# A recurrent kernel on one core: another order of loads, splits and first products in its opening

## The chip, the cores and the metric

The kernel runs on one core of a Trainium2 chip. A core has a matrix engine (TensorE, PE in the profile; PEld is its weight load), a vector engine (VectorE, DVE), a scalar engine (ScalarE, ACT), GpSimd (POOL) and SyncE (SP), which here only issues DMAs. The engines run side by side, each through its own instructions in order, and wait for each other by semaphores. The 16 DMA engines carry all transfers.

The metric is the device time of one execution in microseconds. The time before is 3092.99 us, the median of three runs (3092.69 to 3093.82).

## The reference

```python
xW = einsum('ntd,dh->nth', x, Wx) + b            # N=64 rows, T=256 steps, D=H=1024
h[t] = tanh(h[t-1] @ Wh + xW[t])                 # h[-1] = cond
x = x + h                                        # layer 0
s = silu(cond @ W1.T + b1)
gate = sigmoid(s @ W2.T + b2)                    # one gate per row and column
# layer 1: a Haar transform over t, each of its coefficients times gate, and back; + residual twice
y = x + (x + haar_back(haar(x) * gate))
```

The gate does not depend on t, so the transform and its inverse cancel and y = (x + h) * (2 + gate). This is what the kernel computes, all in float32.

## The kernel before, in words

**The recurrence.** The 256 steps depend on each other. Each step is one 64x1024 by 1024x1024 product with Wh, done as seven products of half size (Strassen's scheme in Winograd's form, `h_product`). Its factors on the side of Wh are four blocks as loaded and three differences: T5 (`first`), T6 (`second`, needs T5), T4 (`others`), and for the seventh product a difference T7 written over a block of Wh in place (`others` too, ahead of T4). They are built once, at step 0. In a step the order on TensorE is products 1, 2, 5, 6, 7, 4, 3, so T5, T6, T7 and T4 are needed in this order.

**The inputs' product.** x @ Wx is done for two steps (a pair, 128 rows) at a time. Float32 matmuls are slow, so x and Wx are split: high bits (x0, w0), the rest (x1, w1), and a mixed part (x2, w2), where x2 = x0 - 4096 x1 and likewise for w. Three products of the fast type fp32r, x0 w0 and x1 (4096 w1) into the banks `main`, x2 w2 into the banks `mixed`, together give the full one. `split_weight` makes the three parts of one 128x1024 block of Wx on VectorE and ScalarE: VectorE masks the high bits (line 118), subtracts them from the raw block in place (135) and makes w2 (137); ScalarE copies w0 (134) and scales w1 (136). `XWork` does the same for a pair of x, and holds the products: `block` for pair 1, block of Wx by block, and `first` and `second` for the later pairs. `take_mixed` brings `mixed` out of PSUM on ScalarE and adds the bias on GpSimd; `finish` adds `main` on VectorE (line 336) and sends the sum through DRAM to the layout of the steps (`xw`); `put` copies one step's `xw` into the bank in which the step accumulates (line 230, ScalarE).

**The opening.** Steps 0 and 1 have no pair product to lean on: `x_block` multiplies pair 0 by the raw Wx (plain float32, four column groups of 32), `h_block` adds cond @ Wh for step 0. Since `x_block(k)` reads the raw block k, the subtraction in place in `split_weight(k)` has to wait for it. Before that come four matmuls on a tile of zeros (`WARM`, line 380) that use no input. Around these stand the gate's first product, cond @ W1.T, in eight blocks (`plain_product` into `gate_ps`), and its second, from step 3 on.

**Who sets the order.** TensorE's order is the program's. Up to the end of step 1, VectorE's and ScalarE's orders are the program's too (`in_order`). SyncE and GpSimd are ordered by the scheduler of the framework. Tiles are reused: the raw blocks 0 to 5 of Wx, then the blocks 0 to 5 of W1, then T5, T6 and T4 lie in the same six tiles in turn (`sums_tile`). So a block of W1 is loaded when the raw block is done with, and a T is made when the gate's product with the block of W1 under it is done. A bank or tile with one buffer (`high`, `sum`, `acc`) is written again when its last reader is done; `hT` has two.

**Order on TensorE at the opening**: x_block 0 to 7, with block 0 of pair 1 after x_block 3 and block 1 after x_block 5; h_block 0 to 7; blocks 2 to 6 of pair 1; gate blocks 0 and 1; block 7; gate blocks 2 to 5; step 1's products 1, 2, 5, 6, 7; gate blocks 6 and 7; products 4, 3; then pair 2's `first`; then step 2.

Of the kernel before, what the change touches and what calls it, by code (L numbers as in the profile page):

```python
# [52 lines left out]
F32 = mybir.dt.float32  # L53
F32R = mybir.dt.float32r
I32 = mybir.dt.int32
AF = mybir.ActivationFunctionType
ALU = mybir.AluOpType

N, T, D = 64, 256, 1024
P = 128  # L60
R = 32
Q = P // R
B = D // P
G = N // R
F = D // Q
# [3 lines left out]
S = 2  # L69
NP = T // S  # L70
HALF = 512
HIGH = -(1 << 12)
UP = float(1 << 12)
DOWN = 1.0 / UP
WARM = 4
LATE = 3
AHEAD = 2
RINGS = 1024
# [3 lines left out]
def tile_cond_resid(  # L82
# [13 lines left out]
    nc = tc.nc  # L96
# [3 lines left out]
    split = ctx.enter_context(tc.tile_pool(name="split", bufs=1))  # L100
# [11 lines left out]
    def load_x(i: int) -> None:  # L112
        pairs[i] = slab(f"x{i}")
        nc.sync.dma_start(out=pairs[i], in_=xT[i])

    def high_bits(v, name: str):
        t = split.tile([P, D], I32, tag="high", name=name)
        nc.vector.tensor_scalar(out=t, in0=v.bitcast(I32), scalar1=HIGH, scalar2=None, op0=ALU.bitwise_and)
        return t[:].bitcast(F32)
# [4 lines left out]
    def load_weight(k: int):  # L124

        raw = sums_tile(f"wx{k}") if k < 3 * KB // 2 else slab(f"wx{k}")
        nc.sync.dma_start(out=raw, in_=wx[k])  # L127
        return raw

    def split_weight(raw, k: int) -> list:  # L130

        w0 = high_bits(raw[:], f"wx_high{k}")
        three = [wpool.tile([P, D], F32R, tag=f"wx{i}", name=f"wx{i}_{k}") for i in range(3)]
        nc.scalar.copy(three[0], w0)
        nc.vector.tensor_sub(raw, raw, w0)
        nc.scalar.activation(three[1], raw, AF.Copy, scale=UP)
        nc.vector.scalar_tensor_tensor(out=three[2], in0=raw, scalar=-UP, in1=w0, op0=ALU.mult, op1=ALU.add)
        return three

    def load_bias(v: bass.AP, pool, tag: str, name: str):  # L140
# [11 lines left out]
    class StrassenWeight:  # L152
# [20 lines left out]

            self.new(6, self.sides[3], self.sides[5])

        def others(self) -> None:

            b = self.sides
            for k in range(KB):
                nc.vector.tensor_sub(self.b12[k], b[3][k], self.b12[k])  # L180
            self.new(4, b[2], b[6])

    def strassen_product(out, a, i: int, first: bool = False) -> None:

# [13 lines left out]
    def plain_product(ps, vT, w, k: int, of=None, start: bool = True, stop: bool = True) -> None:  # L198

        for g in range(G):  # L200
            col = of(g) if of else (g * B + k) * R
            for q in range(Q):


                nc.tensor.matmul(  # L205
                    out=ps[q * R : (q + 1) * R, g * F : (g + 1) * F],
                    lhsT=vT[:, col : col + R],
                    rhs=w[:, q * F : (q + 1) * F],
                    start=start and k == 0 and g == 0,
                    stop=stop and k == B - 1,  # L210
                    skip_group_check=True,
                    tile_position=(0, q * R),
                )
# [19 lines left out]
    def h_product(acc, a: dict, t: int):  # L233

        m16, m57 = (bank(f"m{i}", f"m{i}_{t}") for i in (16, 57))
        m16, m5, m7 = m16[:, :E], m57[:, :E], m57[:, E : 2 * E]
        part = [acc[:, i * E : (i + 1) * E] for i in range(3)]
        y = sums.tile([P, 4, E], F32, tag="y", name=f"y{t}")
        u = sums.tile([P, E], F32, tag="u", name=f"u{t}")
        strassen_product(m16, a[1], 1, True)  # L240
        nc.scalar.copy(y[:, 0], m16)
        strassen_product(part[0], a[2], 2)
        strassen_product(m5, a[5], 5, True)
        strassen_product(m16, a[6], 6)
        nc.scalar.copy(u, m16)
        strassen_product(m7, a[7], 7)
        if t == 1:

            for k in range(B - 2, B):
                plain_product(gate_ps, h0T, w1[k], k)  # L250
        nc.vector.tensor_add(  # L251
            y[:, 1:3], m57[:, : 2 * E].rearrange("p (i e) -> p i e", i=2), u[:].unsqueeze(1).broadcast_to((P, 2, E))
        )
        nc.vector.tensor_add(y[:, 3], m7, y[:, 1])
        strassen_product(part[2], a[4], 4)
        strassen_product(part[1], a[3], 3)
        h = work.tile([P, W], F32, tag="h", bufs=1, name=f"h{t}")
        for v in pieces(t):
            nc.vector.tensor_add(h[:, v], acc[:, v], flat(y)[:, v])  # L259
        return h  # L260
# [6 lines left out]
    def bank(tag: str, name: str):  # L267
        return one_pool.tile([P, HALF], F32, tag=tag, name=name)

    def x_matmul(acc, v, which: int, h: int, k: int, start=False, stop=False) -> None:  # L270

        nc.tensor.matmul(  # L272
            out=acc[h],
            lhsT=v[:, k * P : (k + 1) * P],
            rhs=wx_s[k][which][:, h * HALF : (h + 1) * HALF],
            start=start and k == 0,
            stop=stop and k == B - 1,
        )

    class XWork:  # L280


        def __init__(self, i: int):

            self.i, x = i, pairs[i]
            self.high = high_bits(x[:], f"x_high{i}")
            self.x1 = split.tile([P, D], F32R, tag="x1", name=f"x1_{i}")
            nc.vector.tensor_sub(self.x1, x, self.high)  # L288
            self.x2 = split.tile([P, D], F32R, tag="x2", name=f"x2_{i}")
            nc.vector.scalar_tensor_tensor(  # L290
                out=self.x2, in0=self.x1[:].bitcast(F32), scalar=-UP, in1=self.high, op0=ALU.mult, op1=ALU.add
            )
# [22 lines left out]

        def first(self) -> None:
            self.begin()
            for h in range(2):
                for k in range(B):
                    x_matmul(self.mixed, self.x2, 2, h, k, True, True)  # L320
            self.take_mixed()
            for k in range(B):
                x_matmul(self.main, self.x1, 1, 0, k, start=True)

        def second(self) -> None:
            for k in range(B):
# [27 lines left out]

    h0T = const.tile([P, W], F32, tag="h0T", name="h0T")
    b_row = const.tile([P, D], F32, tag="b_row", name="b_row")
    load_x(1)
    pairs[0] = slab("x0")
    for part in (slice(0, HALF), slice(HALF, D)):
        nc.sync.dma_start(out=pairs[0][:, part], in_=xT[0][:, part])  # L360
        if part.start == 0:
            wx_raw = [load_weight(0)]
    wx_raw += [load_weight(k) for k in range(1, B)]
    nc.sync.dma_start(out=h0T, in_=condT)
    wx_s, wh_raw = [], []
    for k in range(B):
# [8 lines left out]
    in_order.enter_context(tc.manual_schedule(engines={mybir.EngineType.DVE, mybir.EngineType.Activation}))  # L375

    idle = const.tile([P, W], F32, tag="spare", name="idle")
    nc.gpsimd.memset(idle, 0.0)
    for _ in range(WARM):
        nc.tensor.matmul(out=bank("m16", "unused")[:, :F], lhsT=idle[:, :P], rhs=idle[:, :F], start=True, stop=True)  # L380
    now = XWork(1)
    now.begin()
    acc, acc1, gate_ps = bank("acc", "acc0"), bank("m57", "acc1_raw"), bank("gate", "gate_ps1")

    def x_block(k: int) -> None:
# [8 lines left out]
    def load_w1(k: int) -> None:  # L394
        w1.append(sums_tile(f"w1_{k}") if k < 3 * KB // 2 else slab(f"w1_{k}"))
        nc.sync.dma_start(out=w1[k], in_=w1T[k])

    def split_block(k: int) -> None:
        wx_s.append(split_weight(wx_raw[k], k))

    for k in range(B):
        x_block(k)
        split_block(k) if k < B - 1 else None
        if k in (3, 5):
            now.block(k // 4)
    for k in range(B - 1):
        load_w1(k)
    for k in range(B):
        h_block(k)
# [19 lines left out]
    def blocks(v):  # L429
        return v[:].rearrange("p (g b m) -> p g b m", g=G, b=B)  # L430
# [5 lines left out]
    def of_step(x, s: int):  # L436
        return x[:].rearrange("p (b s g m) -> p s g b m", b=B, s=S, g=G)[:, s]
# [31 lines left out]
    for t in range(T):  # L469
# [11 lines left out]
        if t == 0:  # L481
            acc = bank("acc", "acc1")
            nc.vector.tensor_add(acc, acc1, b_n)
            split_block(B - 1)
            load_w1(B - 1)
            for k in range(2, B):
                if k == B - 1:
                    for j in range(2):
                        plain_product(gate_ps, h0T, w1[j], j)
                now.block(k)  # L490
            now.take_mixed()
            wh_s = StrassenWeight(wh_raw)
            wh_s.first()
            wh_s.second()
            xw_next = now.finish()
            for k in range(2, B - 2):
                plain_product(gate_ps, h0T, w1[k], k)
            wh_s.others()
            later = XWork(2)


        elif s == 0:
            if i + 1 < NP:
                acc = put(xw[1], t + 1)
            if i + 2 < NP:
                now.second()
                if i + 3 < NP:
                    later = XWork(i + 2)
                xw_next = now.finish()
        if s == 1 and i + 3 < NP:  # L510
            now = later
# [18 lines left out]


        x = pairs[i]
        if t + S < T:
            nc.gpsimd.tensor_add(of_step(x, s), of_step(x, s), blocks(hT))  # L534
        if LATE <= t < LATE + B:
            k = t - LATE
# [78 lines left out]
```

## Time and profile before

| | us |
|---|---|
| median of three runs | 3092.99 |
| the profiled execution | 3094.69 |
| its span, from the first to the last instruction | 3092.8 |
| TensorE busy in the span | 3081.2 |
| VectorE busy | 1769.1 |
| step 1's first product starts at | 48.52 |
| pair 2's `first` starts on TensorE at | 59.05 |
| step 2's first product starts at | 64.75 |

The span starts at the first instruction of the core; all times below count from there. In a timeline each line is one group of like instructions: start, duration, engine, line of the kernel, operation, tile written, tiles read, shape and count, and in brackets the idle time of the engine before the group and what ended it. A float32 matmul appears as two records. TensorE is busy for all but some 12 us of the span, so what a change to the opening can alter is the time at which step 2 starts; from there on both programs have the same order on TensorE.

### The profile page before, as it was taken

Reading aid. Unit: us, or ns where it says so; the run is one execution under the profiler, and the core shown is the slowest. Engines: PE = TensorE matmul, PEld = TensorE weight load, DVE = VectorE, ACT = ScalarE, POOL = GpSimd, SP = SyncE. Lnnn points to the kernel's source line nnn. Section 1 sums busy time; section 2 is a strip of 40 time slices with the busy share of each in tenths; the row PEclk is TensorE's granted clock in tenths of the full one; section 3 lists DMA queues with packets and bytes.
Section 4 is the critical chain, followed back from the end, with each engine's and each line's share of the span. In section 5 each row is a group of like instructions: output and inputs, shape, how many; then the busy total and the mean of one; then the engine's idle time right before and its main releaser. Section 6 shows DMA issues by size and latency. Waiting matters only on the chain.

```text
span 3092.8 us, 138217 instructions
## 1 busy us (share of the span) xinstructions
PE 3081.2 (100%) x64072; PEld 2693.9 (87%) x64072; DVE 1769.1 (57%) x2739; ACT 713.7 (23%) x1420; POOL 1109.4 (36%) x765
## 2 busy tenths in 40 slices
PE   9999999999999999999999999999999999999999
PEld 6888888888888888888888888888888888888888
DVE  7555556555555555555555555555555555555556
ACT  3222222222222222222222222222222222222221
POOL 1233433343333343433333333333333333333332
PEclk9999999999999999999999999999999999999999
DMA  7332232232232322222222222222222222222221
GB/s 253 118 111 94 94 103 92 92 103 98 91 101 88 105 91 99 91 96 84 92 90 96 86 91 91 91 91 91 90 92 91 90 92 90 92 88 90 95 78 57
DMA packets 164034, 299.13 MB, mean 97 GB/s; under 512 B 44160, under 2 KB 110208, under 8 KB 163456
## 3 DMA queue, kind: packets, MB, share of 16 engines
q1 hardware_dynamic: 163168, 290.03, 27.3%
q8 instruction: 501, 8.21, 1.1%
q14 instruction: 77, 0.63, 0.1%
q10 hardware_dynamic: 288, 0.26, 0.0%
HBM read 154.40 MB, written 135.79 MB: 94 GB/s over the span
## 4 chain that ended last, share of the span: by engine, by line
PE 96%; DMA 2%; DVE 1%; SPq 0%; issue 0%; ACT 0%; DVEq 0%; ACTq 0%
PE main L272 30%; PE m L188 29%; PE acc L188 21%; PE mixed L272 15%; DMA w<-w1T 0%; PE acc L205 0%; DMA wh<-wh 0%; DMA wx<-wx 0%; DMA sum_d<-sum 0%; PE gate_ps L205 0%; DMA xw<-sum_d 0%; DMA b_n<-b 0%; DVE x L288 0%; SPq L127 0%; DVE hT L478 0%
## 5 line engine op out<-in xcount | busy, mean ns | idle before, releaser
L534 POOL TENSOR_TENSOR x<-x,hT 128x512 f32<-128x512 f32 x254 | 450.6, 1774 | 1751.6 <-DVE hT L478 1730.6
L272 PE MATMUL main<-wx,x 128*128 128x512 f32 x4032 | 973.4, 393 | 0.0
L272 PEld LDWEIGHTS main<-wx,x 128*128 128x128 f32 x4032 | 746.9, 188 | 177.0 <-issue 25.6
L251 DVE TENSOR_TENSOR y<-m,u 128x256 f32<-128x256 f32 x255 | 108.2, 424 | 847.8 <-PE m L188 847.8
L272 PE MATMUL mixed<-wx,x 128*128 128x512 f32 x2016 | 495.2, 397 | 1.6 <-DVE x L290 1.6
L188 PE MATMUL m<-t,s 128*32 128x128 f32 x16320 | 492.5, 273 | 0.2 <-DVE s L220 0.2
L272 PEld LDWEIGHTS mixed<-wx,x 128*128 128x128 f32 x2016 | 368.7, 188 | 98.8 <-issue 24.6
L188 PEld LDWEIGHTS m<-t,s 128*32 128x32 f32 x16320 | 450.8, 110 | 0.5 <-issue 0.4
L305 POOL TENSOR_TENSOR sum<-sum,b_row 128x512 f32<-128x512 f32 x252 | 325.3, 1292 | 197.3 <-ACT sum L304 197.3
L477 ACT ACTIVATE h<-h 128x512 f32<-128x512 f32 (+1 forms) x258 | 162.0, 629 | 794.9 <-DVE h L259 793.3
L440 POOL TENSOR_TENSOR x<-x,factor 128x512 f32<-128x512 f32 x244 | 330.5, 1354 | 15.4 <-DVE factor L426 5.7
L259 DVE TENSOR_TENSOR h<-acc,y 128x512 f32<-128x512 f32 (+1 forms) x257 | 176.5, 688 | 236.5 <-PE acc L188 236.3
L478 DVE STREAM_TRANSPOSE hT<-h 128x512 f32<-128x512 f32 (+1 forms) x258 | 182.4, 708 | 202.5 <-ACT h L477 202.5
L188 PEld LDWEIGHTS m<-wh,hT 128*32 128x32 f32 x8160 | 208.7, 109 | 87.3 <-issue 83.8
L290 DVE SCALAR_TENSOR_TENSOR x<-x,x_high 128x1024 fp32r<-128x1024 f32 x126 | 282.7, 2244 | 0.1
L188 PE MATMUL m<-wh,hT 128*32 128x128 f32 x8160 | 275.5, 275 | 0.0
L188 PE MATMUL acc<-wh,s 128*32 128x128 f32 x8160 | 271.1, 273 | 0.4 <-issue 0.4
L188 PE MATMUL m<-wh,s 128*32 128x128 f32 x8160 | 270.1, 273 | 0.4 <-DVE wh L180 0.4
L188 PE MATMUL acc<-t,hT 128*32 128x128 f32 x8160 | 270.2, 273 | 0.2 <-issue 0.2
L188 PE MATMUL acc<-wh,hT 128*32 128x128 f32 x8160 | 269.8, 273 | 0.3 <-ACT acc L230 0.2
L296 ACT CAST x<-x_high 128x1024 fp32r<-128x1024 f32 x126 | 131.9, 1047 | 465.4 <-PE main L272 462.5
L188 PEld LDWEIGHTS acc<-wh,s 128*32 128x32 f32 x8160 | 228.9, 110 | 1.1 <-issue 1.1
(59 smaller groups left out, 2354.0 us busy)
## 6 DMA issues: line engine op xcount, KB each, us to landing
x<-xT SPq DMA_DIRECT2D x127, 512.0 KB, 3.7
sum_d<-sum SPq DMA_DIRECT2D x126, 512.0 KB, 3.1
xw<-sum_d SPq DMA_DIRECT2D x1008, 64.0 KB, 2.0
yT<-x SPq DMA_DIRECT2D x122, 512.0 KB, 3.5
wx<-wx SPq DMA_DIRECT2D x8, 512.0 KB, 8.7
wh<-wh SPq DMA_DIRECT2D x8, 512.0 KB, 10.2
w<-w1T SPq DMA_DIRECT2D x8, 512.0 KB, 7.2
w<-w2T SPq DMA_DIRECT2D x8, 512.0 KB, 4.4
```

What stands on the lines that cost most here:

```text
L188: nc.tensor.matmul(out=out[q * R : (q + 1) * R], lhsT=a[:, k * R : (k + 1) * R], rhs=wh_s.sides[i][k][:, q], start=first and k == 0, stop= ...
L251: nc.vector.tensor_add(y[:, 1:3], m57[:, : 2 * E].rearrange("p (i e) -> p i e", i=2), u[:].unsqueeze(1).broadcast_to((P, 2, E)))
L259: nc.vector.tensor_add(h[:, v], acc[:, v], flat(y)[:, v])
L272: nc.tensor.matmul(out=acc[h], lhsT=v[:, k * P : (k + 1) * P], rhs=wx_s[k][which][:, h * HALF : (h + 1) * HALF], start=start and k == 0, s ...
L290: nc.vector.scalar_tensor_tensor(out=self.x2, in0=self.x1[:].bitcast(F32), scalar=-UP, in1=self.high, op0=ALU.mult, op1=ALU.add)
L296: nc.scalar.copy(self.x0, self.high)
L305: nc.gpsimd.tensor_add(s, s, b_row[:, h * HALF : (h + 1) * HALF])
L440: nc.gpsimd.tensor_mul(of_step(x, s), of_step(x, s), blocks(factor))
L477: nc.scalar.activation(h[:, v], h[:, v], AF.Tanh)
L478: nc.vector.transpose(hT[:, v], h[:, v])
L534: nc.gpsimd.tensor_add(of_step(x, s), of_step(x, s), blocks(hT))
```

## The change

It touches the opening only, in these parts.

- `split_weight` writes w - w0 to the tile of w1 and not over the raw block; the scaling by 4096 is then done in place on that tile, after w2 has been made from it.
- The loads start with block 0 of Wx, issued by ScalarE, and a quarter of pair 0 (before: a half) by SyncE; then block 1 of Wx, the rest of pair 0, pair 1, and the blocks 2 to 7 of Wx.
- The matmuls on zeros are five of 128 columns (before: four of 256), and VectorE writes the zeros (before: GpSimd).
- VectorE and ScalarE split block 0 of Wx first, then pair 1, then blocks 1 to 7; before, pair 1 came first and block 7 after step 0.
- All eight blocks of W1 are loaded ahead of b1 (before: the eighth after it).
- Gate blocks 0 to 3 stand ahead of block 7 (before: 0 and 1), 4 and 5 behind it (before: 2 to 5); 6 and 7 stay inside step 1.
- VectorE makes pair 2's high bits ahead of T5, then T5, T6, T7, then pair 1's sum (`finish`), then T4, then the rest of pair 2's split. Before: T5, T6, `finish`, T7, T4, the whole split.
- `first` of pair 2 begins with the eight matmuls of x1 into `main`, then the sixteen into `mixed`; before, and for all later pairs, it is the other way round.
- GpSimd's additions of h to x for steps 0 and 1 both stand at step 1. In the built order they follow the sums of pair 2, and the store of pair 0 moves behind five loads of b2.

```diff
-WARM = 4
+WARM = 5
...
-        nc.sync.dma_start(out=raw, in_=wx[k])
+        (nc.sync if k else nc.scalar).dma_start(out=raw, in_=wx[k])
...
         nc.scalar.copy(three[0], w0)
-        nc.vector.tensor_sub(raw, raw, w0)
-        nc.scalar.activation(three[1], raw, AF.Copy, scale=UP)
-        nc.vector.scalar_tensor_tensor(out=three[2], in0=raw, scalar=-UP, in1=w0, op0=ALU.mult, op1=ALU.add)
+        nc.vector.tensor_sub(three[1], raw, w0)
+        w1 = three[1][:].bitcast(F32)
+        nc.vector.scalar_tensor_tensor(out=three[2], in0=w1, scalar=-UP, in1=w0, op0=ALU.mult, op1=ALU.add)
+        nc.scalar.activation(three[1], w1, AF.Copy, scale=UP)
...
-        def others(self) -> None:
+        def third(self) -> None:
 
             b = self.sides
             for k in range(KB):
                 nc.vector.tensor_sub(self.b12[k], b[3][k], self.b12[k])
-            self.new(4, b[2], b[6])
+
+        def fourth(self) -> None:
+
+            self.new(4, self.sides[2], self.sides[6])
...
             self.high = high_bits(x[:], f"x_high{i}")
+
+        def split(self) -> None:
+
+            i, x = self.i, pairs[self.i]
             self.x1 = split.tile([P, D], F32R, tag="x1", name=f"x1_{i}")
...
         def first(self) -> None:
             self.begin()
+
+            def low() -> None:
+                for k in range(B):
+                    x_matmul(self.main, self.x1, 1, 0, k, start=True)
+
+
+            low() if self.i == 2 else None
             for h in range(2):
                 for k in range(B):
                     x_matmul(self.mixed, self.x2, 2, h, k, True, True)
             self.take_mixed()
-            for k in range(B):
-                x_matmul(self.main, self.x1, 1, 0, k, start=True)
+            low() if self.i > 2 else None
...
-    load_x(1)
+    wx_raw = [load_weight(0)]
     pairs[0] = slab("x0")
-    for part in (slice(0, HALF), slice(HALF, D)):
+    for part in (slice(0, 2 * P), slice(2 * P, D)):
         nc.sync.dma_start(out=pairs[0][:, part], in_=xT[0][:, part])
         if part.start == 0:
-            wx_raw = [load_weight(0)]
-    wx_raw += [load_weight(k) for k in range(1, B)]
+            wx_raw.append(load_weight(1))
+    load_x(1)
+    wx_raw += [load_weight(k) for k in range(2, B)]
...
-    nc.gpsimd.memset(idle, 0.0)
+    nc.vector.memset(idle[:, :P], 0.0)
     for _ in range(WARM):
-        nc.tensor.matmul(out=bank("m16", "unused")[:, :F], lhsT=idle[:, :P], rhs=idle[:, :F], start=True, stop=True)
-    now = XWork(1)
-    now.begin()
+        nc.tensor.matmul(out=bank("m16", "unused")[:, :P], lhsT=idle[:, :P], rhs=idle[:, :P], start=True, stop=True)
...
     for k in range(B):
         x_block(k)
-        split_block(k) if k < B - 1 else None
+        split_block(k)
+        if k == 0:
+            now = XWork(1)
+            now.split()
+            now.begin()
         if k in (3, 5):
             now.block(k // 4)
-    for k in range(B - 1):
+    for k in range(B):
         load_w1(k)
...
             nc.vector.tensor_add(acc, acc1, b_n)
-            split_block(B - 1)
-            load_w1(B - 1)
             for k in range(2, B):
                 if k == B - 1:
-                    for j in range(2):
-                        plain_product(gate_ps, h0T, w1[j], j)
+                    for j in range(4):
+                        gate_block(j)
                 now.block(k)
             now.take_mixed()
+            for k in range(4, B - 2):
+                gate_block(k)
+            later = XWork(2)
             wh_s = StrassenWeight(wh_raw)
             wh_s.first()
             wh_s.second()
+            wh_s.third()
             xw_next = now.finish()
-            for k in range(2, B - 2):
-                plain_product(gate_ps, h0T, w1[k], k)
-            wh_s.others()
-            later = XWork(2)
-
+            wh_s.fourth()
+            later.split()
...
-        if t + S < T:
+        if t == 0:
+            hT0 = hT
+        elif t == 1:
+
+            for r, v in enumerate((hT0, hT)):
+                tc.keep_in_program_order(nc.gpsimd.tensor_add(of_step(x, r), of_step(x, r), blocks(v)))
+        elif t + S < T:
             nc.gpsimd.tensor_add(of_step(x, s), of_step(x, s), blocks(hT))
```

`gate_block(k)` is `plain_product(gate_ps, h0T, w1[k], k)` under a name of its own.

More of the change, by code (lines that the diff above doesn't have):

```diff
@@ L399, in split_block, with gate_block @@
         wx_s.append(split_weight(wx_raw[k], k))
+    def gate_block(k: int) -> None:
+        plain_product(gate_ps, h0T, w1[k], k)
     for k in range(B):
         x_block(k)
-        split_block(k) if k < B - 1 else None
+        split_block(k)
[3 more added lines that the diff above has]
+            now.begin()
         if k in (3, 5):
             now.block(k // 4)
-    for k in range(B - 1):
+    for k in range(B):
         load_w1(k)
@@ L483, in tile_cond_resid @@
             nc.vector.tensor_add(acc, acc1, b_n)
-            split_block(B - 1)
-            load_w1(B - 1)
             for k in range(2, B):
                 if k == B - 1:
-                    for j in range(2):
-                        plain_product(gate_ps, h0T, w1[j], j)
+                    for j in range(4):
+                        gate_block(j)
                 now.block(k)
             now.take_mixed()
+            for k in range(4, B - 2):
+                gate_block(k)
+            later = XWork(2)
             wh_s = StrassenWeight(wh_raw)
@@ L494, in tile_cond_resid @@
             wh_s.second()
+            wh_s.third()
             xw_next = now.finish()
-            for k in range(2, B - 2):
-                plain_product(gate_ps, h0T, w1[k], k)
-            wh_s.others()
-            later = XWork(2)
+            wh_s.fourth()
+            later.split()
         elif s == 0:
@@ L508, in tile_cond_resid @@
                     later = XWork(i + 2)
+                    later.split()
                 xw_next = now.finish()
```

## The prediction, made before the changed kernel ran

> **What bounds the kernel now.** The page comes first: TensorE is busy for 3081.2 of 3092.8 us, and the chain that ended last is 96% TensorE. From step 2 on a pair of steps takes 25.64 us of unbroken matmuls while the gate's second product runs (`mixed` at 109.05, then 134.69) and 23.87 after it (185.97, 209.84), and the change leaves that order alone. So I read only the opening, by the timelines of TensorE and VectorE, then ScalarE's, and ask one thing: when does step 2's first product start? Before, that is 64.75.
>
> TensorE's timeline:
>
> ```profile
> PE 3081.2 (100%) x64072; PEld 2693.9 (87%) x64072; DVE 1769.1 (57%) x2739; ACT 713.7 (23%) x1420; POOL 1109.4 (36%) x765
> ...
> 7.51 1.94 PE L205 MATMUL acc<-wx,x 128*32 128x256 f32 x16 [1.14 <-DMA wx<-wx]
> 9.19 1.97 PE L205 MATMUL acc_raw<-wx,x 128*32 128x256 f32 x16
> ...
> 13.68 1.05 PE L205 MATMUL acc<-wx,x 128*32 128x256 f32 x16
> ...
> 48.52 1.06 PE L188 MATMUL m<-wh,hT 128*32 128x128 f32 x32
> ...
> 53.52 0.43 PE L188 MATMUL m<-wh,s 128*32 128x128 f32 x8 [0.18 <-DVE wh L180]
> 53.76 1.91 PE L205 MATMUL gate_ps<-w,h0T 128*32 128x256 f32 x32
> ...
> 59.05 3.96 PE L272 MATMUL mixed<-wx,x 128*128 128x512 f32 x16 [1.63 <-DVE x L290]
> ...
> 64.75 1.08 PE L188 MATMUL m<-wh,hT 128*32 128x128 f32 x32
> ```
>
> Four losses: the first product waits for wx until 7.51; up to 13.0 a group of 16 takes 1.70 us, from then on 0.86, a slow clock that costs 13.68 - 7.51 - 4 x 0.865 = 2.71; the seventh product (52.01 to 53.76) takes 1.75 in place of 0.87, as T7 comes late (0.88); pair 2's `first` waits for its split (59.05 against 57.28: 1.77). VectorE shows why the last two are late:
>
> ```profile
> 11.21 1.23 DVE L135 TENSOR_TENSOR wx<-wx,wx_high 128x1024 f32<-128x1024 f32 x1 [2.99 <-PE acc_raw L205]
> ...
> 34.67 0.69 DVE L443 TENSOR_TENSOR h<-acc,b_n 128x512 f32<-128x512 f32 x1 [0.71 <-PE acc L205]
> ...
> 46.18 3.68 DVE L166 TENSOR_TENSOR t<-wh,t 128x512 f32<-128x512 f32 x4 [0.95 <-PE gate_ps L205]
> 49.78 1.27 DVE L336 SCALAR_TENSOR_TENSOR sum<-main,sum 128x512 f32<-128x512 f32 x2
> 50.98 2.48 DVE L180 TENSOR_TENSOR wh<-wh,wh 128x512 f32<-128x512 f32 x4
> 53.38 2.49 DVE L166 TENSOR_TENSOR t<-wh,t 128x512 f32<-128x512 f32 x4
> ```
>
> It idles 2.99 for x_block 0 and 0.95 for gate blocks 2 and 3 (T6's tiles), and is otherwise full to 59.0. So there are two chains to re-time, TensorE's and VectorE's.
>
> **The change, part by part.**
>
> *First product.* It needs block 0 of Wx and the first part of x0. Before, 1.31 MB stood in the queue up to it; by the DMA view 1.32 MB had moved at 6.0, and it landed at 1.65 + 5.7 = 7.4. Now 0.66 MB is needed. Lower bound: nothing else is served meanwhile; 0.50 MB had moved at 3.5 and 0.69 at 4.0, and pair 1's 0.52 MB landed at 4.2, 0.7 after its bytes: about 4.5. Upper bound: the other queue's backlog is served as well, and it stays at 7.5. I take the middle, 6.0: a gain of 1.5. The Trainium skill, "DMA: Bandwidth & Descriptors" (Issuing engines are not separate DMA queues), speaks against more: queues of different engines share the same 16 DMA engines and interleave. By it block 0 shares evenly with SyncE's stream, about 1.05 MB moves first, and the landing would be an estimated 5.9 to 6.6. No row shows two loading queues at once.
>
> *Slow clock.* Zero matmuls from 1.31 to 6.37 did not lift it; it lifted 5.5 us after the first real one. I keep 5.5, a cost of 2.71. Bounds: 0 if the five matmuls (about 0.85 us each, half of the old 1.28 plus the same weight load) now join the real ones without a gap and count; if it takes 11.7 us from the first zero matmul, as before (1.31 to 13.0), then from 1.0 to 12.7, which is 6.7 us or 3.3 of cost. The skill's "TensorE: Matmul & The Clock Gate" (Part 1) has a window of about 3.4 us that runs freely, so 3.4 to 6.8 us of slow clock, cost 1.7 to 3.4, different each run; its middle would take 0.15 off the sum.
>
> *TensorE from there.* From first product to step 1's first product was 48.52 - 7.51 = 41.01. The new order has the same blocks and gate blocks in it, so 6.0 + 41.0 = 47.0. Gate blocks 0 to 3 start around 40.1; block 3 of W1 was issued at 34.11 and took 7.6, landing at 41.7, needed at 42.7: covered by 1.0. The eight loads of W1 follow the same queue as before. If the cover goes, step 1 starts no earlier than 45.95 (41.7 + 0.87 + 1.58 + 1.75). Then products 1, 2, 5, 6, 7: 4.36 without the stall; gate blocks 6, 7: 1.72; products 4, 3: 1.80; `first`: 5.70. Step 2 at 47.0 + 13.58 = 60.6.
>
> *VectorE.* Block 0's split runs 6.0 to 9.4 (period 3.38), no longer waiting for x_block 0; raw is not written, so the 2.99 goes. Pair 1's x is now fifth in the queue with 2.1 MB, where block 1 of Wx was, which landed at 2.59 + 6.7 = 9.3: no wait. 3.3 for pair 1, seven splits 23.7: 36.4. The split of block 7, after step 0 before, now lies ahead of it, so h follows at 36.4 and not 34.67; nobody but VectorE's own successors needs it before 47. ScalarE's last scaling (36.4 to 37.4) stands ahead of tanh in its queue: 0.3 late, tanh 37.4. From tanh to the sides' end 2.5 (GpSimd's addition, which stretched one to 1.38, is gone): 39.9; acc 0.6; pair 2's high bits 0.7; T5 from 41.2, 2.4; T6 from 43.6, 3.6 (the old row, 3.68, in which GpSimd adds the bias; gate blocks 2, 3 are done by 43.6); T7 47.2 to 49.6; `finish` 1.2; T4 50.8 to 53.3; x1 54.5; x2 55.7. TensorE wants the end of T7 at 51.2, of T4 at 53.75, x1 at 54.9, x2 at 56.8. All are met, with 0.4 to spare at T4 and x1. Were they late, TensorE would lose just that.
>
> *`first` turned round.* It gives x2 1.9 us more. Its price: `mixed` is now last, and ScalarE takes it and then puts step 2's accumulator in order. In before the second half's copy started at 63.05 and the put ended at 64.13, 1.28 us after `first` left `mixed` (62.85), hidden under the 1.90 of x1. Now step 2's first product covers 0.90 and its second needs the accumulator: a new wait of about 0.4. Between 0 (`put` hidden by some slack in the records) and 1.1 (both copies still to do, 1.09 in the row at 44.46). I take 0.45.
>
> *The rest, at nothing.* GpSimd's two additions come after pair 2's sums, ending near 65; the transposes of steps 2 and 3 now wait for them, as hT has two buffers, and step 2's comes at about 68: 3 us of cover; without it the lateness goes straight to TensorE, with the sides behind it in VectorE's queue. The store of pair 0 goes out near 65, ahead of the load of pair 4 at some 67 (before 68.91), wanted a pair later. `finish` ends at 50.8, before 51.05: the transfer to `xw` took until 60.4 and stays below `put` at 60.6. Zeros by VectorE: under the wait for data.
>
> Sum: 1.5 + 0.88 + 1.77 = 4.2 (64.75 - 60.6), less 0.45: 3.75. The profiled execution would go from 3094.69 to 3090.9; the median of before lies 1.7 lower, at 3092.99, so 3089.2.
>
> **The rivals.**
>
> *A, everything early.* Data at 4.5, clock free: TensorE would reach W1 block 3 first and stand until 41.7: step 1 at 45.95, step 2 at 59.5, and VectorE must lose its 1.2 of GpSimd contention in T6 as well. Gain 5.2 - 0.45 = 4.8: 3088.2. For it: the bounds above. Against: VectorE at 36.4, tied to pair 1's x at 9.3.
>
> *B, the start gains nothing.* Block 0 lands at 7.4 as before, behind shared traffic. Then only 0.88 + 1.77 - 0.45 = 2.2 come off: 3090.8. For it: the queue's 0.7 to 1.4 us of lag between bytes and landing. Against: half the bytes.
>
> *C, slower.* ScalarE's queue starves: SyncE keeps the engines full (1.02 share from 7.5 on), and block 0 of Wx takes what a load in a full queue takes, 10.2 us (the page's wh). Landing 0.75 + 10.2 = 11, first product 5.0 later than 6.0, VectorE's chain as late: 3094.2. It decides from a landing of 9.7; beyond 0.2% only from 16. Against: the first 4 us moved only 0.69 MB, so the engines have room.
>
> **How the numbers follow.** Main case 0.6, A 0.16, B 0.18, C 0.04, others 0.02. 0.2% is 6.2 us, about what a measurement of this kernel can tell from no change; A, B, C and the main case all lie within it. To pass it on the fast side, block 3 of W1, pair 1's x and the clock must all be over 1 us earlier: 0.08. Slow side: C far beyond its row, or a late GpSimd addition: 0.03. Range: from A with 1.2 more (no contention) to B with the wait at 1.1 and 0.6 of clock: 3087.0 to 3092.0.
>
> **What would show it.** First x_block near 6.0; its groups at 1.70 for about 5.5 us; no idle of VectorE at line 135; h at 36.4; T7 and T4 ahead of TensorE; `first` without idle; a gap of about 0.4 before product 2 of step 2; step 2 at 60.6. It is wrong if VectorE's 36.4 is late by over 0.4, or W1 lands later than before.

## The result and the profile after

The changed kernel takes 3088.96 us, the median of 22 runs (3087.58 to 3092.66), beside 3093.33 for the kernel before (22 runs, 3090.64 to 3096.45). The ratio is 0.9986, with a 95% interval of 0.998 to 0.9993: 4.4 us less. The interval does not contain 1, so the kernel did become faster, but by little: 0.07% to 0.2%, where the forecast had named 0.2% as about what can be told from no change. The forecast was 3089.2 in 3087.0 to 3092.0.

The profiled execution took 3089.96 us, its span 3088.2, which is 4.6 less than before. The point to read is the start of step 2's second product, behind all that the change touches: 60.77, before 65.65, so 4.88 earlier. What follows it took 3027.4 us in this profile and 3027.15 in that of before.

The changed kernel's page and its TensorE timeline (start, duration, engine, line, operation and tiles, shape, count, idle time before and its cause):

```profile
span 3088.2 us, 138210 instructions
```

```profile
1.05 4.21 PE L394 MATMUL unused<-idle 128*128 128x128 f32 x10 [1.05 <-DVE idle L392]
5.19 1.94 PE L209 MATMUL acc<-wx,x 128*32 128x256 f32 x16
6.90 1.88 PE L209 MATMUL acc_raw<-wx,x 128*32 128x256 f32 x16
8.61 1.04 PE L209 MATMUL acc<-wx,x 128*32 128x256 f32 x16
9.48 1.04 PE L209 MATMUL acc_raw<-wx,x 128*32 128x256 f32 x16
...
45.12 1.06 PE L192 MATMUL m<-wh,hT 128*32 128x128 f32 x32
...
51.21 0.65 PE L192 MATMUL acc<-t,hT 128*32 128x128 f32 x16
52.03 0.42 PE L192 MATMUL acc<-t,hT 128*32 128x128 f32 x8 [0.18 <-DVE t L167]
52.64 0.43 PE L192 MATMUL acc<-t,hT 128*32 128x128 f32 x8 [0.18 <-DVE t L167]
52.88 1.06 PE L192 MATMUL acc<-wh,s 128*32 128x128 f32 x32
53.87 2.11 PE L275 MATMUL main<-wx,x 128*128 128x512 f32 x8
55.81 3.79 PE L275 MATMUL mixed<-wx,x 128*128 128x512 f32 x16
59.53 1.08 PE L192 MATMUL m<-wh,hT 128*32 128x128 f32 x32
60.77 1.08 PE L192 MATMUL acc<-wh,hT 128*32 128x128 f32 x32 [0.17 <-ACT acc L234]
```

The first product now starts at 5.19, right behind the zeros. Only two groups run at 1.71 us before the step falls to 0.87. The trace's own clock record shows that this is the clock: its first interval at full speed begins at 8.60 here and at 13.01 in the kernel before. Ahead of it the trace has no record, and the page's `PEclk` counts such time as full speed. Step 1 starts at 45.12. Product 4 (`acc<-t`) takes 1.67 in place of 0.87: it is the one that stalls now, on T4. `first` follows without a gap, and step 2's second product comes 1.24 behind the first where 0.90 is its pace.

VectorE's timeline of the changed kernel, and GpSimd's:

```profile
5.13 0.69 DVE L118 TENSOR_SCALAR wx_high<-wx 128x1024 int32<-128x1024 int32 x1 [4.13 <-DMA wx<-wx]
...
8.77 0.69 DVE L118 TENSOR_SCALAR x_high<-x 128x1024 int32<-128x1024 int32 x1 [0.43 <-DMA x<-xT]
...
35.03 0.69 DVE L462 TENSOR_TENSOR h<-acc,b_n 128x512 f32<-128x512 f32 x1
...
42.18 2.48 DVE L167 TENSOR_TENSOR t<-wh,t 128x512 f32<-128x512 f32 x4
44.59 2.49 DVE L181 TENSOR_TENSOR wh<-wh,wh 128x512 f32<-128x512 f32 x4
48.24 0.69 DVE L349 SCALAR_TENSOR_TENSOR sum<-main,sum 128x512 f32<-128x512 f32 x1 [1.17 <-POOL sum L312]
49.49 0.69 DVE L349 SCALAR_TENSOR_TENSOR sum<-main,sum 128x512 f32<-128x512 f32 x1 [0.55 <-POOL sum L312]
50.10 2.48 DVE L167 TENSOR_TENSOR t<-wh,t 128x512 f32<-128x512 f32 x4
```

```profile
43.46 5.99 POOL L312 TENSOR_TENSOR sum<-sum,b_row 128x512 f32<-128x512 f32 x2 [43.02 <-ACT sum L311]
```

T6 and T7 run at their full pace, 2.48 each. But GpSimd's two additions of the bias, 2.97 before, now take 5.99, and `finish` waits 1.17 + 0.55 = 1.72 for them, with T4 queued behind it. This wait was not in the forecast.

### The profile page after: what moved, and what is told of

Its sections match the earlier page's. It is cut to its first block, busy times and chain, and to the rows that moved or that the text cites. A ratio compares the mean times of both kernels' runs of the same rounds, so it can differ in the third digit from the quotient of the medians.

```text
span 3088.2 us, 138210 instructions
## 1 busy us (share of the span) xinstructions
PE 3078.7 (100%) x64074; PEld 2693.5 (87%) x64074; DVE 1762.0 (57%) x2740; ACT 712.1 (23%) x1420; POOL 1110.6 (36%) x764
## 4 chain that ended last, share of the span: by engine, by line
PE 99%; DVE 0%; DMA 0%; POOL 0%; SPq 0%; ACT 0%; issue 0%; DVEq 0%; ACTq 0%
PE main L275 30%; PE m L192 30%; PE acc L192 22%; PE mixed L275 16%; PE acc L209 1%; PE gate_ps L209 0%; PE acc_raw L209 0%; POOL sum L312 0%; DMA sum_d<-sum 0%; PE unused L394 0%; SPq L359 0%; DMA b_n<-b 0%; DVE hT L497 0%; ACT h L496 0%; DVE s L224 0%
```

## The experiments

Each edit is against the changed kernel. A run without a ratio is one profiled execution. In these the time of the whole execution says little: what follows step 2's second product took between 3024.4 and 3028.3 us in the fourteen profiles, mostly by stray pauses of 0.3 to 1.0 at scattered places. So they are compared by the start of step 2's second product (60.77 in the changed kernel) and the rows ahead of it.

**What makes the start early.** First, who issues block 0 of Wx:

```diff
-        (nc.sync if k else nc.scalar).dma_start(out=raw, in_=wx[k])
+        nc.sync.dma_start(out=raw, in_=wx[k])
```

> Only edit: SyncE, not ScalarE, issues block 0 of Wx, still as the first load. Theory 'fewer bytes ahead': the first x_block starts as in the changed kernel, at 5.2, plus at most the 0.45 of one more issue on SyncE (5.2 to 5.7). Rival 'second queue': without it the block again waits in line and x_block starts near 7. Pair 1's x should land within 0.5 of 8.6 by both, so VectorE's h stays at 35.0 to 35.6 and the time of step 2's second product at 60.8 to 61.5.

VectorE's and TensorE's timelines of this kernel:

```profile
4.31 0.69 DVE L118 TENSOR_SCALAR wx_high<-wx 128x1024 int32<-128x1024 int32 x1 [3.31 <-DMA wx<-wx]
...
9.63 0.69 DVE L118 TENSOR_SCALAR x_high<-x 128x1024 int32<-128x1024 int32 x1 [2.11 <-DMA x<-xT]
```

```profile
5.19 1.94 PE L209 MATMUL acc<-wx,x 128*32 128x256 f32 x16
...
61.65 1.08 PE L192 MATMUL acc<-wh,hT 128*32 128x128 f32 x32 [0.17 <-ACT acc L234]
```

The first x_block starts at 5.19, as in the changed kernel, so the second queue is not what makes it early. Block 0 even lands 0.8 sooner (4.31 against 5.13), which TensorE cannot use, as it is still at its zeros. The second queue does something else: pair 1's x is there at 8.8 with it and at 9.6 without, which moves VectorE's whole chain (h at 35.90, before 35.03) and the second product to 61.65. That miss (pair 1's x within 0.5 was expected) is the finding: ScalarE's issue is worth 0.9, through pair 1. About half of it can be SyncE's own time: with one issue less ahead, it issues pair 1 at 2.11 and not 2.59. The page "DMA: Bandwidth & Descriptors" (Issuing engines are not separate DMA queues) of the Trainium skill, which the forecast weighed, holds as far as block 0 goes: it lands later when SyncE's stream is interleaved with it.

Then the order itself:

```diff
-    wx_raw = [load_weight(0)]
+    load_x(1)
     pairs[0] = slab("x0")
-    for part in (slice(0, 2 * P), slice(2 * P, D)):
+    for part in (slice(0, HALF), slice(HALF, D)):
...
-            wx_raw.append(load_weight(1))
-    load_x(1)
-    wx_raw += [load_weight(k) for k in range(2, B)]
+            wx_raw = [load_weight(0)]
+    wx_raw += [load_weight(k) for k in range(1, B)]
```

(with all loads on SyncE)

> Only edit: the loads stand in the before kernel's order again, all on SyncE (pair 1 of x, half of pair 0, block 0 of Wx, the rest of pair 0, blocks 1 to 7). Theory 'the load order is the whole gain at the start, one to one on both chains': block 0 lands near 7.4, first x_block at 7.5 (from 5.2), VectorE's first split at 7.4, pair 1's split without a wait behind it, h at about 37.3 (from 35.0, idle of 0.43 saved), T4's end near 54.5, step 2's second product near 62.7 in place of 60.8. Rival 'the first product's time hides under VectorE's chain or W1': step 2's second product within 0.5 of 60.8.

TensorE's timeline:

```profile
7.86 1.94 PE L209 MATMUL acc<-wx,x 128*32 128x256 f32 x16 [2.60 <-DMA wx<-wx]
...
63.06 1.08 PE L192 MATMUL acc<-wh,hT 128*32 128x128 f32 x32 [0.17 <-ACT acc L234]
```

The first product comes 2.7 later; VectorE's first split starts at 7.74, 2.6 later, of which 0.4 is made up by the idle ahead of pair 1's split, now gone. The other 2.3 reach the end undiminished, through VectorE: h at 37.31, T4's end at 54.86, the second product 2.3 later. This run has undone the second queue as well; against the run before, the order alone is worth 1.4 (63.06 against 61.65).

**The zeros and the slow clock.**

```diff
-WARM = 5
+WARM = 0
...
-    nc.vector.memset(idle[:, :P], 0.0)
```

> Only edit: the five matmuls on zeros and their memset are left out (they take no part in the result). Theory 'the zeros that run up to the first real matmul shorten the slow clock': the slow stretch after the first x_block grows from 3.4 to about 5.5 or more (the before kernel, with a gap of 1.14, had 5.5), and step 1 starts on TensorE at 46.2 or later in place of 45.1. Rival 'the zeros do nothing, and the length depends on where the execution falls': between 3.4 and 6.8 whatever the zeros, so 3.4 again is possible. In either case T4 sets the end of step 1 as long as step 1 starts before 46.0, and step 2's second product stays at 60.8.

TensorE's timeline:

```profile
4.89 1.94 PE L209 MATMUL acc<-wx,x 128*32 128x256 f32 x16 [4.89 <-DMA wx<-wx]
...
60.70 1.08 PE L192 MATMUL acc<-wh,hT 128*32 128x128 f32 x32 [0.16 <-ACT acc L234]
```

The first product starts at 4.89 and the clock lifts 2.6 us later, sooner than the 3.4 of the changed kernel; step 1 at 44.72, second product at 60.70. With 16 products of 1.71 slow and 0.865 fast, the length of the slow stretch can be worked out from the group in which the step changes. With the zeros it comes out, over the kernels of this study, between 2.0 and 4.8 us. The shortest is in the run with `mixed` first, further down; its TensorE timeline:

```profile
6.90 1.15 PE L209 MATMUL acc_raw<-wx,x 128*32 128x256 f32 x16
7.88 1.04 PE L209 MATMUL acc<-wx,x 128*32 128x256 f32 x16
...
10.10 1.07 PE L209 MATMUL acc<-wx,x 128*32 128x256 f32 x16 [0.32 <-DMA wx<-wx]
```

The group at 6.90 takes 0.98: slow for t with t + (1.71 - t)/2 = 0.98, so 0.25, and 1.71 + 0.25 = 2.0 since 5.19 (the trace's clock record has 1.93). The changed kernel run again had 4.8. Without the zeros there are two samples, 2.6 and 3.8, inside that spread. So the stretch differs from execution to execution. A use of the zeros is not shown, but two samples cannot exclude one either: the four shortest stretches, 1.9 to 2.6, all have zeros ahead of them.

The row at 10.10 shows a limit: when the clock lifts this early, TensorE stands ahead of x_block 2 until its block of Wx is there. In this run and the two others that began at 5.19 and had under 2.4 us of slow clock, step 1 starts at 44.96 to 45.07, against 45.12 in the changed kernel with its 3.4. So with these loads a shorter slow stretch gained next to nothing.

**VectorE's chain: the split that leaves the raw block whole.**

```diff
-        nc.vector.tensor_sub(three[1], raw, w0)
-        w1 = three[1][:].bitcast(F32)
-        nc.vector.scalar_tensor_tensor(out=three[2], in0=w1, scalar=-UP, in1=w0, op0=ALU.mult, op1=ALU.add)
-        nc.scalar.activation(three[1], w1, AF.Copy, scale=UP)
+        nc.vector.tensor_sub(raw, raw, w0)
+        nc.scalar.activation(three[1], raw, AF.Copy, scale=UP)
+        nc.vector.scalar_tensor_tensor(out=three[2], in0=raw, scalar=-UP, in1=w0, op0=ALU.mult, op1=ALU.add)
```

> Only edit: split_weight subtracts over the raw block again, as in the before kernel. Theory 'this edit frees VectorE's chain': the subtraction of block 0 waits for x_block 0's end (about 8.6, idle near 2.8), pair 1's split begins at 11.5 and not 8.8, h at 37.7, T4 ends near 55.2 if GpSimd is shut out alike, and step 2's second product at about 63.4 in place of 60.8. Rival 'pair 1's x sets VectorE's start anyhow': h stays at 35.0 and the second product at 60.8.

VectorE's and then TensorE's timeline:

```profile
8.65 1.23 DVE L135 TENSOR_TENSOR wx<-wx,wx_high 128x1024 f32<-128x1024 f32 x1 [2.58 <-PE acc_raw L208]
```

```profile
63.70 0.54 PE L191 MATMUL acc<-wh,hT 128*32 128x128 f32 x12 [0.17 <-ACT acc L233]
```

The wait for x_block 0 is back with 2.58, h comes at 37.99, 3.0 later, and the second product 2.9 later (2.6 was expected): the largest share of any part undone alone.

**GpSimd's additions.** One run takes them off GpSimd, for pair 1 alone:

```diff
                 nc.scalar.activation(s, self.mixed[h], AF.Copy, scale=-DOWN)
-                nc.gpsimd.tensor_add(s, s, b_row[:, h * HALF : (h + 1) * HALF])
+                if self.i > 1:
+                    nc.gpsimd.tensor_add(s, s, b_row[:, h * HALF : (h + 1) * HALF])
...
+                if self.i == 1:
+                    nc.vector.tensor_add(v, v, b_row[:, h * HALF : (h + 1) * HALF])
```

> Only edit: for pair 1 the bias is added by VectorE in finish (two more operations of 0.6) and not by GpSimd. Theory 'GpSimd was shut out by VectorE's unbroken T6 and T7, and finish then waited 1.72 for it': finish starts without idle at about 47.0, T4 ends at 51.9 in place of 52.6, TensorE's stall in product 4 falls from 0.8 to 0.1 or 0.2, step 2's second product at 60.1 in place of 60.8. Rival 'VectorE's chain is too long in itself': T4 ends at 52.6 or later and the stall stays 0.8.

Another puts VectorE at rest earlier:

```diff
+            xw_next = now.finish()
             wh_s.third()
-            xw_next = now.finish()
             wh_s.fourth()
```

> Only edit: pair 1's finish stands ahead of T7 again, as in the before kernel. Theory 'GpSimd is shut out as long as VectorE runs without a break': VectorE now comes to rest after T6 at 44.7, GpSimd's first addition ends 1.1 later, at 45.8, the two together take about 3.5 from 43.5 and not 6.0; finish ends near 47.7, T7 at 50.1, T4 at 52.5. Product 7 stalls by about 0.9, product 4 no more than 0.2, and step 2's second product stays within 0.3 of 60.8. Rival 'these two additions take 6 us by themselves': they end at 49.4 again, finish ends at 50.1, T7 at 52.5, T4 at 54.9, and step 2's second product comes near 63.

GpSimd's, VectorE's and TensorE's timelines of the kernel with `finish` ahead of T7:

```profile
43.49 3.64 POOL L312 TENSOR_TENSOR sum<-sum,b_row 128x512 f32<-128x512 f32 x2 [43.05 <-DMA w<-w1T]
```

```profile
45.93 0.69 DVE L349 SCALAR_TENSOR_TENSOR sum<-main,sum 128x512 f32<-128x512 f32 x1 [1.18 <-POOL sum L312]
```

```profile
61.08 1.08 PE L192 MATMUL acc<-wh,hT 128*32 128x128 f32 x32 [0.16 <-ACT acc L234]
```

GpSimd asks at the same time, 43.49, but is done after 3.64 and not 5.99: its first addition ends 1.1 after VectorE has come to rest, as it does in the changed kernel. So the additions do not take 6 us by themselves; they are shut out while VectorE runs T6 and T7 in one piece. The rival falls. The order of `finish` and T7 is worth 0.3: the same 1.73 of waiting now holds up T7, product 7 takes 1.92, and product 4 no longer stalls.

With the bias on VectorE `finish` starts without idle, at 47.24; VectorE's and TensorE's timelines:

```profile
47.24 0.69 DVE L350 SCALAR_TENSOR_TENSOR sum<-main,sum 128x512 f32<-128x512 f32 x1
...
49.90 2.49 DVE L167 TENSOR_TENSOR t<-wh,t 128x512 f32<-128x512 f32 x4
```

```profile
45.80 1.06 PE L192 MATMUL m<-wh,hT 128*32 128x128 f32 x32
...
51.89 1.06 PE L192 MATMUL acc<-t,hT 128*32 128x128 f32 x32
...
60.66 1.08 PE L192 MATMUL acc<-wh,hT 128*32 128x128 f32 x32 [0.17 <-ACT acc L234]
```

Product 4 runs through without a stall. Still the second product comes only 0.1 sooner (0.7 was expected), since in this execution the slow clock lasted 4.8 us and TensorE itself reached step 1 at 45.80, 0.7 late. The two chains are that close: T4 hides a long slow stretch, and a long slow stretch hides T4. Of the expected 0.7 for T4 itself, 0.2 is seen (52.39 against 52.58), as T5 too began 0.24 late: 0.1 of it came down VectorE's chain, the rest fits the gate's first block, which ended later.

**Gate blocks 2 and 3 behind block 7 again.**

```diff
-                    for j in range(4):
+                    for j in range(2):
                         gate_block(j)
...
-            for k in range(4, B - 2):
+            for k in range(2, B - 2):
                 gate_block(k)
```

> Only edit: gate blocks 2 and 3 stand behind block 7 again, as in the before kernel. TensorE's sum to step 1 is unchanged (45.1). VectorE's T6 stands on the tiles under gate blocks 2 and 3, which now end near 42.4 and 43.3. Theory 'the order of the gates matters little once TensorE is early': T6's first half starts within 0.3 of 42.2 and its second 0.2 to 0.5 later, a break of VectorE in which GpSimd may get in; T4 within 0.8 of 52.6 on either side. Rival 'T6 waits as before for 0.95': T6 0.9 later, T4 at 53.4, second product at 61.6.

GpSimd's, VectorE's and TensorE's timelines:

```profile
41.61 3.01 POOL L312 TENSOR_TENSOR sum<-sum,b_row 128x512 f32<-128x512 f32 x2 [41.17 <-ACT sum L311]
```

```profile
39.90 3.58 DVE L167 TENSOR_TENSOR t<-wh 128x512 f32<-128x512 f32 x4
43.40 3.58 DVE L167 TENSOR_TENSOR t<-wh,t 128x512 f32<-128x512 f32 x4
```

```profile
61.18 1.08 PE L192 MATMUL acc<-wh,hT 128*32 128x128 f32 x32 [0.17 <-ACT acc L234]
```

T4 ends at 52.98 and the second product comes at 61.18, both 0.4 later. The order of the gates matters that little, but by another way than either theory had it: block 7 is done sooner, so GpSimd asks at 41.61, inside T5. There it gets in at once, and T5 and T6 each become 1.1 longer, a little less than one addition takes alone (1.28). `finish` then waits for nothing. T6 did not wait for the gates. The Trainium skill's page "SBUF — State Buffer" (SBUF: two separate sides) has a port pair that VectorE and GpSimd share as an exclusive lock, held for a whole instruction by whoever starts first; the steps of 1.1 agree with it. That GpSimd can lose several instructions in a row the traces show: in the changed kernel it asked at 43.46, within T6, and five more of VectorE's instructions ran ahead of it; why it gets in during T5 (here and in the run with the raw block overwritten) and not during T6 is left open.

**`first` turned round.**

```diff
-            low() if self.i == 2 else None
...
-            low() if self.i > 2 else None
+            low()
```

> Only edit: pair 2's first has the order of the before kernel again, mixed ahead of x1. Theory 'the turn takes away a wait for x2 and buys a smaller one at the accumulator': first now waits for x2 until about 55.0 (from 53.8, 1.2 idle), step 2's first product at 60.7 in place of 59.5, and the wait of 0.37 ahead of its second product is gone, so the second product comes at 61.6 in place of 60.8: the turn is worth 0.8. Rival 'it only moves the wait': second product at 60.8 again, worth 0.

TensorE's timeline:

```profile
55.11 3.92 PE L275 MATMUL mixed<-wx,x 128*128 128x512 f32 x16 [1.09 <-DVE x L297]
...
61.67 1.06 PE L192 MATMUL acc<-wh,hT 128*32 128x128 f32 x32
```

1.09 of waiting for x2 is back, the wait at step 2's second product is gone, and the sum is 0.9 for the turn, as expected.

**The accumulator between the two copies.**

```diff
         for h in range(2):
             s = self.sum[:, h * HALF : (h + 1) * HALF]
+            if h and between:
+                between()
             nc.scalar.activation(s, self.mixed[h], AF.Copy, scale=-DOWN)
```

(`between` puts step 2's accumulator, at step 1 alone)

> Only edit: on ScalarE, step 2's accumulator is put between the two copies of pair 2's mixed banks and no more behind both. Theory 'the put behind the second copy is the new wait of step 2': its second product no longer waits (0.37 gone) and comes 0.87 after the first, at 60.4 in place of 60.8, as xw landed at 58.9. Rival 'the wait is for xw or for the bank': the wait stays at 0.3 or more.

TensorE's timeline:

```profile
59.68 1.08 PE L192 MATMUL m<-wh,hT 128*32 128x128 f32 x32
60.58 1.06 PE L192 MATMUL acc<-wh,hT 128*32 128x128 f32 x32
```

The second product follows 0.90 behind the first, at TensorE's own pace: the wait was for the order on ScalarE and nothing else. It comes at 60.58 and not 60.4, as T4 ended 0.15 later in this execution (52.73), and step 2's first product with it.

**Putting them together, with the changed kernel timed beside them on the same chip.** First the bias on VectorE and the accumulator between the copies:

> Two edits: pair 1's bias on VectorE, and step 2's accumulator put between pair 2's two copies. Theory 'TensorE and VectorE are level at T4': with both, T4 no longer stalls TensorE and the 0.37 at step 2 is gone, so step 2's second product comes at 59.6 to 60.3, by how long the slow clock lasts in that execution (2.0 to 5.5 us so far). The ratio to the before kernel is 0.9982 to 0.9986, about 0.5 to 1 us under the changed kernel's time. Rival 'it all ends elsewhere': the same time as the changed kernel.

Then, besides these two, no zeros, and block 1's split ahead of pair 1's:

```diff
         split_block(k)
-        if k == 0:
+        if k == 1:
             now = XWork(1)
             now.split()
             now.begin()
-        if k in (3, 5):
-            now.block(k // 4)
+        if k in (4, 6):
+            now.block(k // 2 - 2)
```

> Four edits: the two of the run before, no matmuls on zeros (they take no part in the result), and block 1 of Wx split ahead of pair 1's x, with pair 1's blocks 0 and 1 behind x_block 4 and 6. Theory: VectorE's 0.4 of idle for pair 1's x goes and T4 ends near 51.6; the first product comes at 4.9; TensorE alone sets step 2, whose second product comes at 58.9 to 60.0 by the length of the slow clock. Ratio to the before kernel 0.9980 to 0.9985, 1 to 1.5 us under the changed kernel. Rival 'pair 1's split is now late for its block 0': a stall of up to 1 us behind x_block 4, and no gain over the two edits.

And the changed kernel:

> The changed kernel once more, beside the two variants on the same chip. Both theories: first x_block at 5.2, h at 35.0, T4's end near 52.6, step 2's second product near 60.8, whether the slow clock lasts 2 or 5 us, since T4 sets it up to a stretch of about 5; ratio to the before kernel 0.998 to 0.9993.

| kernel | median of 11 | range | ratio to before | interval |
|---|---|---|---|---|
| two edits | 3087.89 | 3086.93 to 3089.21 | 0.9983 | 0.9974 to 0.9992 |
| four edits | 3089.90 | 3087.22 to 3091.57 | 0.9988 | 0.9979 to 0.9997 |
| changed kernel again | 3089.68 | 3088.47 to 3091.28 | 0.999 | 0.9981 to 0.9999 |

TensorE's timelines, of the two edits and then of the four:

```profile
52.25 0.43 PE L192 MATMUL acc<-t,hT 128*32 128x128 f32 x8 [0.17 <-DVE t L167]
...
60.05 1.06 PE L192 MATMUL acc<-wh,hT 128*32 128x128 f32 x32
```

```profile
5.28 1.94 PE L209 MATMUL acc<-wx,x 128*32 128x256 f32 x16 [5.28 <-DMA wx<-wx]
...
51.51 1.06 PE L192 MATMUL acc<-t,hT 128*32 128x128 f32 x32
...
59.93 1.06 PE L192 MATMUL acc<-wh,hT 128*32 128x128 f32 x32
```

The second products come as expected: 60.05 and 59.93. With four edits the way there does not: the first product comes at 5.28 and not 4.9, and T4 ends at 52.00 and not 51.6. The changed kernel's second product is at 61.08, 0.3 later than expected: its slow stretch of 4.8 us reached T5, which waited 0.22 for the gate. Product 4 still stalls a little with two edits (clock lifted early, after 2.0 us) and not at all with four. By the times of whole executions, the two edits are the best version seen, 1.8 us under the changed kernel where 0.5 to 1 was expected: nine of their eleven times lie under the lowest of the changed kernel's, though the intervals of the ratios overlap. For the four edits the expected gain of 1 to 1.5 us did not come. Their eleven times fall in two groups, five from 3087.2 to 3088.7 and six from 3089.9 to 3091.6; the profile is of one in the lower group, so what the upper ones lose was not seen. A longer slow clock without the zeros would fit, but it was not shown.

## Why the prediction was right

The kernel became 4.4 us faster by the medians, 3.75 were forecast, and 3088.96 lies in the range, near the point of 3089.2. As in the forecast, TensorE runs on unchanged after step 2's start. The two losses that it set out to remove, behind T7 and ahead of `first`, are gone at their size. But several other terms were off, and they cancelled in part: that the time lies so near the point is luck. Point by point, us gained at step 2's second product, from the rows of both profiles:

| term | forecast | measured |
|---|---|---|
| first product (6.0; 5.19) | 1.5 | 2.32 |
| from there to step 1 (41.0; 39.93), the slow clock in the main | 0 | 1.08 |
| product 7 no longer waits for T7 | 0.88 | 0.88 |
| product 4 waits for T4 | 0 | -0.79 |
| `first` no longer waits for its split | 1.77 | 1.70 |
| step 2's second product waits for `put` | -0.45 | -0.34 |
| the rest | 0 | 0.03 |
| sum | 3.70 | 4.88 |

- *First product.* The middle of two bounds, 6.0, was taken; it came at 5.19, nearer the lower one. The data were there at 5.1 with the second queue, ahead of the 5.9 to 6.6 that the forecast had estimated from even sharing, and at 4.3 with one queue.
- *Slow clock.* The step that kept 5.5 us "as before" took one draw for a constant. In this study it was 2.0 to 5.5; the changed kernel's profile had 3.4, which is 1.0 less of cost. The Trainium skill's page "TensorE: Matmul & The Clock Gate" (Part 1) has a window of about 3.4 us that runs freely, and so a stretch that differs each run; that agrees. The 2.0 and 2.6 seen are shorter than a window, which the 3.4 to 6.8 worked out from it in the forecast had excluded.
- *TensorE to step 1.* The sum of 41.0 holds: 5.19 + 41.0 - 1.0 = 45.2, measured 45.12. (The bound for a late block 3 of W1 adds up to 45.90, not 45.95.) The gate blocks 0 to 3 found their blocks of W1 loaded.
- *VectorE.* Its start was right (the 2.99 is gone) and h came 1.4 sooner than 36.4: pair 1's split began at 8.77 and not 9.4, and a split takes 3.30 and not 3.38. (Of the profile before, "otherwise full to 59.0" passes over two waits of 0.7 around h.) From there the step that failed is T6 with 3.6 "in which GpSimd adds the bias", and `finish` at once. T6 took 2.48, and the cost came back as a wait of 1.72 at `finish`. T4's end at 52.6 instead of 53.3 follows from h, T6 and `finish` together.
- *"All are met, with 0.4 to spare".* At T4 this failed: TensorE came 1.9 earlier than forecast and T4 only 0.7. The wait at `finish` decided it: without its 1.72 T4 would have ended near 50.9 (an estimate, 52.58 - 1.72), ahead of the 51.9 at which product 4 needs its last part. The text named T4 and x1 as the tightest, and said that TensorE would lose just the lateness; it did, 0.8. Of the signs that the forecast listed two failed: T4 ahead of TensorE and, by the clock, groups at 1.70 for about 5.5 us. The others came as told or earlier.
- *`first` turned round.* Right in mechanism and size: 0.34 for 0.45, and undoing the turn costs 0.9.
- *The parts at nothing.* They stayed there: the transposes of steps 2 and 3 showed no wait for GpSimd, whose two additions ended at 64.1, and `xw` was there before `put`.
- *The rivals.* A (4.8 gained) is the nearest to what happened on TensorE, yet it had the limit in W1's block 3; the limit was T4. B and C did not happen.

## What to carry to other kernels

Where two engines' chains meet, undo each part alone and look at the meeting point: here the parts undone one by one cost 2.9 (the raw block), 2.3 (the loads' order and queue), 0.9 (`first`), 0.4 (the gates) and 0.3 us (`finish`), more than the 4.9 that the whole change gives, since whichever chain is late sets the end. The orders of block 0's and block 7's split, of pair 2's high bits, of W1's eighth block and of the additions of h were not undone alone. Work that shares something with another engine, such as GpSimd's and VectorE's here, has two prices in a forecast, and one of them falls due: a slower step (T5 and T6 1.1 longer each) or a wait further on (1.72 at `finish`). No run here paid both. And an effect that differs between executions, such as the slow clock at the start, is a range in the sum and not a term copied from one profile.

## What the runs showed of the hardware

- GpSimd's additions, two of some 1.3 us, took 3.0 when it got in between VectorE's instructions and 5.6 to 6.3 when it asked while VectorE ran T6 and T7 back to back; in the latter case the first one ended about 1.1 after VectorE's last.
- The slow clock after the first product lasted 2.0 to 5.5 us over the fourteen profiles, 2.0 to 4.8 with five matmuls on zeros right ahead of it, 2.6 and 3.8 with none. The interval at full speed that then begins in the trace's clock record has one of just two lengths in all fourteen, 3075.409 or 3078.822 us, 3.413 apart.
- Issuing one of two early loads from a second queue made that load land 0.8 us later and one that was four places behind land 0.9 us sooner.
- Stray pauses of 0.3 to 1.0 us in the steady part (matmuls that start that much later than like ones) sum to between 0.5 and 3.6 us in the fourteen profiles, the larger of which is near the size of the change itself.
